# First recurrent layer: both gates in one stream, memory by a scan of six terms, state by a pair scan

## The chip, the core and the metric

The kernel runs on one core of a Trainium2 chip. Five engines matter: PE (matrix products), DVE (vector), ACT (activation functions), POOL (a second vector engine) and SP (which only issues DMAs). Each works off its own instructions in order and waits for the others by semaphores. The metric is the device time of one execution in microseconds (us), the median of several runs.

## The reference

Four layers run one after the other on x of shape (8, 512, 512): batch B = 8, time T = 512, width D = 512. Each adds its output to x. The first three are recurrences over the 512 time steps, the fourth is causal attention with 16 heads. The change touches the first layer:

```python
def step(h, x_t):
    fused = jax.nn.sigmoid(jnp.concatenate([x_t, h], axis=-1) @ w_W + w_b)
    hidden_state, output_state = jnp.split(fused, 2, axis=-1)
    memory_state = x_t @ wx_W + wx_b + hidden_state * (h @ wh_W + wh_b)
    h_new = output_state * h + (1.0 - output_state) * jnp.tanh(memory_state)
    return (h_new, h_new)
```

So a step needs three products of the state h with 512x512 matrices: for the hidden gate, for the output gate, and for the memory. The second and third layers are plain: `h = tanh(x_t @ Wx + b + h @ Wh)`.

## The kernel before

All three recurrences run at the same time, each some steps behind the one before (`OFF = (0, 9, 21)`). One call of `turn(s)` is one time step of each layer that is live at s. Layer 0 is live for s = 0 to 511, layer 1 from s = 9, layer 2 from s = 21, and the loop ends at s = 532. The order of the instructions on PE, DVE, ACT and POOL is the program's own (`manual_schedule`); only the loads and the splitting of weights ahead of the loop are ordered by the scheduler.

The state is float32, but these products are made in bf16: a float32 number is the sum of three bf16 numbers, its upper half and two rests. The state tile `h0` therefore holds four slots per number, [128, 4 chunks, 8 batches, 4 slots], of which three are in use: the number, the number less its upper half (`rest`, line 481), and that less its upper half again. The matmul takes the upper halves of all four slots as 32 columns (8 batches x 4 slots), and the weights are split in three bf16 parts too (`split`, lines 352 to 357, which takes two copies on ACT and two subtractions on DVE for each part of a weight). Four products fill four groups of 32 partitions of one PSUM tile.

What a step does, in the order of the program:
- PE: `ph` (48 matmuls of 256 columns: products of the state for the memory and the hidden gate), `po` (48 of 128 columns: for the output gate), `give0` and `give12` (line 508 and 521: products of x for a coming step), `p12` (48 of 256 columns: the state products of layers 1 and 2), and, from about s = 85 on, three `pieces` of the attention's projections (line 630).
- Layer 0 on DVE, ACT and POOL (lines 720 to 745): `turned` (line 590) transposes `ph` in 32x32 blocks from PSUM to SBUF, so that the four slots' products lie side by side; a fifth number beside them is the bias or x's share; `summed` (line 596) adds the five. A sigmoid gives the hidden gate (736). The same for `po`: `turned`, `summed` into `so`, a sigmoid into `og` (739). A scan over pairs (728) makes memory = gate x sum + x's share; it runs along the row as state = gates x state + term, and a gate of 0 starts each pair anew. Then a tanh (741), `keep` = og x h on POOL (742), `drop` = (og - 1) x tanh on DVE (743), the new state = keep - drop (744), and `rest` twice (481).
- POOL: `place` for the next step (551 twice for layer 0, 555 for layers 1 and 2) adds the biases to x's shares, and 752 adds the new state to x.
- Layers 1 and 2: `turned` of `p12` and `summed` on DVE (behind `rest` of layer 0), four tanh on ACT (763), `rest` on POOL (481), and two additions on POOL (773), the last of them into `xo`.

In POOL's order the additions 773 of one step are followed by `keep` of the next, then by its 551, 551, 555, 752. Every fourth step, `given` (538) transposes the shares of x for the next four steps on DVE.

Of the kernel before, what the change touches and what calls it, by code (L numbers as in the profile page):

```python
# [9 lines left out]
F32 = mybir.dt.float32  # L10
BF16 = mybir.dt.bfloat16
AF = mybir.ActivationFunctionType
ALU = mybir.AluOpType
# [10 lines left out]
NS = 5  # L24
# [10 lines left out]
def cond_residual_kernel(  # L35
# [292 lines left out]
    with ExitStack() as rec:  # L328
# [13 lines left out]
        v0o = wpool.tile([P, KC, 3, D], BF16, name="v0o")  # L342
# [49 lines left out]
        for c in range(KC):  # L392
            stage = stages[c % 3]
            w, r = stage[:, 0 : 3 * D], stage[:, 3 * D :]
            load_rows(nc.sync, w[:, 0:D], wh_w, c)
            load_rows(nc.sync, w[:, D : 2 * D], w_w[D:, 0:D], c)
            load_rows(nc.scalar, w[:, 2 * D :], w_w[D:, D:], c)
            split(v0[:, c], w[:, 0 : 2 * D], r[:, 0 : 2 * D], nc.vector)
            split(v0o[:, c], w[:, 2 * D :], r[:, 2 * D :], nc.vector)
# [40 lines left out]
        s0, s12 = [], []  # L440
        for i in range(2):
            s0.append(wpool.tile([P, 3 * KC, B, NS], F32, name=f"s0_{i}"))
            s12.append(wpool.tile([P, 2 * KC, B, NS], F32, name=f"s12_{i}"))
            nc.vector.tensor_copy(
                s0[i][:, 0:KC, :, NS - 1], bh.unsqueeze(2).to_broadcast([P, KC, B])
            )

        sh = []
        gates = wpool.tile([P, KC, B, 2], F32, name="gates")
        nc.vector.memset(gates, 0.0)
        for i in range(2):
            sh.append(wpool.tile([P, 2 * KC, B, 2], F32, name=f"sh_{i}"))

# [8 lines left out]

        def part(h, i):
            return h[..., i]

        def top(h, i):

            return h.bitcast(BF16)[..., 2 * i + 1]
# [68 lines left out]
        def place(s, layers):  # L540
# [4 lines left out]
            if layers[0] == 0:  # L545
                for to, k in (
                    (s0[s % 2][:, KC:, :, NS - 1], slice(0, 2 * KC)),
                    (sh[s % 2][:, 0:KC, :, 1], slice(2 * KC, 3 * KC)),
# [45 lines left out]
        def summed(to, parts):  # L594

            nc.vector.tensor_reduce(to, parts, AX.X, ALU.add)  # L596
# [103 lines left out]
        def turn(s):  # L700
# [6 lines left out]
            if 0 in now:  # L707
# [3 lines left out]
                stream(po, old0, v0o, 1)  # L711
# [8 lines left out]
            if 0 in now:  # L720
                parts = s0[s % 2]

                def small(name, n=KC):
                    return sp.tile([P, n, B], F32, tag=name, name=f"{name}_{s}")

                def scan(to, q, ab):
                    to, q, ab = (x.rearrange("p c b i -> p (c b i)") for x in (to, q, ab))
                    nc.vector.tensor_tensor_scan(to, q, ab, 0.0, ALU.mult, ALU.add)

                so, og = small("so"), small("og")  # L730
                mem = sp.tile([P, KC, B, 2], F32, tag="mem", name=f"mem_{s}")
                th, keep, drop = small("th"), small("keep"), small("drop")
                hm = sh[s % 2]
                turned(parts[:, 0 : 2 * KC], ph)
                summed(hm[..., 0], parts[:, 0 : 2 * KC])
                nc.scalar.activation(gates[..., 1], hm[:, KC:, :, 0], AF.Sigmoid)  # L736
                turned(parts[:, 2 * KC : 3 * KC], po)
                summed(so, parts[:, 2 * KC : 3 * KC])
                nc.scalar.activation(og, so, AF.Sigmoid)  # L739
                scan(mem, gates, hm[:, 0:KC])  # L740
                nc.scalar.activation(th, mem[..., 1], AF.Tanh)  # L741
                nc.gpsimd.tensor_tensor(keep, og, part(old0, 0), ALU.mult)  # L742
                nc.vector.scalar_tensor_tensor(drop, og, 1.0, th, ALU.subtract, ALU.mult)  # L743
                nc.vector.tensor_tensor(part(new0, 0), keep, drop, ALU.subtract)
# [10 lines left out]
            if later:  # L755
                ps = rows_of(later)
                turned(s12[s % 2][ps], p12[ps])
                s_ = sp.tile([P, 2 * KC, B], F32, tag="s_", name=f"s_{s}")
# [441 lines left out]
```

## Time and profile before

| what | value |
| --- | --- |
| time, median of 3 runs | 3488.78 us (3484.61 to 3498.84) |
| span of the profiled execution | 3484.3 us |
| PE busy | 3313.8 us (95%) |
| PE weight loads busy (beside PE) | 2650.8 us (76%) |
| DVE busy | 2469.7 us (71%) |
| ACT busy | 1434.6 us (41%) |
| POOL busy | 1311.7 us (38%) |
| first transpose of `ph` | 49.71 us |
| last transpose of `ph` (s = 511) | 2656.09 us |

The profile is of one execution. A row of the timeline reads: start, duration, engine, line, operation, output<-inputs, shapes, count, and in brackets how long the engine was idle before and what ended that. A row of the costliest groups gives busy time, mean duration in ns, and idle time ahead of it. Loads and splits fill the first 50 us, the recurrences run from 50 to about 2,700 us, and the rest is attention, which the change does not touch.

### The profile page before, as it was taken

To read this page: it belongs to the slowest core of one execution; us is meant where nothing else is said; L and a number is where in the kernel's file an instruction comes from. 1 tells how busy PE (TensorE), PEld (TensorE's weight loads), DVE (VectorE), ACT (ScalarE), POOL (GpSimd) and SP (SyncE) were. 2 spreads that over 40 slices of the span, in tenths; PEclk is the share of its full clock that TensorE was granted. 3 is DMA by queue.
4 is the path that set the end of the run, shared out by engine and by line. 5 is a ranking of instruction groups with operands and counts; after the bars stand their busy time and mean duration, and the time that the engine had idled before them with its cause. 6 is when DMAs were issued, how large, how long until landed. Compare 5 with 4: busy or idle time off the path is not lost. (4 is left out here: it accounts for less than half of the span.)

```text
span 3484.3 us, 213758 instructions
## 1 busy us (share of the span) xinstructions
PE 3313.8 (95%) x94712; PEld 2650.8 (76%) x94712; DVE 2469.7 (71%) x7411; ACT 1434.6 (41%) x5203; POOL 1311.7 (38%) x4970
## 2 busy tenths in 40 slices
PE   4899999999999999999999999999999879999999
PEld 2677778888888888888888888888886646666666
DVE  4677777777777777777777777777775357777775
ACT  3233333333333333333333333333333257777774
POOL 2444444444444444444444444444443111111110
PEclk9999999999999999999999999999999979999999
DMA  4200000001000100100010001000113121222211
GB/s 128 55 8 8 8 23 17 17 20 29 17 20 18 31 17 17 29 17 17 20 29 17 17 19 29 17 17 17 29 20 64 35 90 47 82 69 65 64 51 26
DMA packets 186565, 114.61 MB, mean 33 GB/s; under 512 B 134220, under 2 KB 165988, under 8 KB 185628
## 3 DMA queue, kind: packets, MB, share of 16 engines
q1 hardware_dynamic: 180056, 96.08, 10.9%
q8 instruction: 743, 12.17, 1.5%
q10 hardware_dynamic: 4992, 2.11, 0.3%
q0 software_dynamic: 592, 2.75, 0.2%
q14 instruction: 182, 1.49, 0.1%
HBM read 59.97 MB, written 40.92 MB: 29 GB/s over the span
## 5 line engine op out<-in xcount | busy, mean ns | idle before, releaser
L565 PEld LDWEIGHTS <-h 128*32 128x32 bf16 x49152 | 1074.0, 97 | 216.6 <-DVE h L481 152.7
L763 ACT ACTIVATE h<-s 64x32 f32<-64x32 f32 x2048 | 537.1, 262 | 1004.9 <-DVE s L596 978.8
L565 PE MATMUL ph<-v,h 128*32 128x256 bf16 x24576 | 796.4, 274 | 59.6 <-DVE h L481 43.8
L581 PE MATMUL p<-v,h 128*32 128x256 bf16 x24576 | 820.2, 273 | 15.6 <-DVE h L481 12.7
L581 PEld LDWEIGHTS <-h 128*32 128x32 bf16 x24576 | 719.5, 97 | 108.7 <-ACT h L763 16.1
L481 POOL TENSOR_TENSOR h<-h 128x64 f32<-128x64 f32 (+1 forms) x1006 | 323.0, 321 | 1152.3 <-ACT h L763 1112.9
L508 PE MATMUL pg<-w0x,xb 128*32 128x384 f32 x4096 | 452.6, 491 | 26.0 <-DMA w0x<-in_wx_W_dram 10.5
L590 DVE STREAM_TRANSPOSE s<-ph 128x256 f32<-128x256 f32 x512 | 230.3, 450 | 346.5 <-PE ph L565 346.4
L565 PE MATMUL po<-v0o,h 128*32 128x128 bf16 x24576 | 469.9, 220 | 6.2 <-issue 5.2
L521 PE MATMUL pg<-w12x,xb 128*32 128x256 f32 x4096 | 349.5, 380 | 9.3 <-DVE raw L538 5.7
L481 DVE TENSOR_TENSOR h<-h 128x32 f32<-128x32 f32 (+1 forms) x1078 | 281.3, 262 | 69.6 <-ACT h L763 32.9
L521 PEld LDWEIGHTS pg<-w12x,xb 128*32 128x32 f32 x4096 | 165.3, 110 | 175.7 <-issue 137.3
L630 PE MATMUL pq<-xo,w_qkv 128*32 128x256 f32 (+2 forms) x4136 | 292.7, 371 | 0.5 <-issue 0.5
L736 ACT ACTIVATE gates<-sh 128x32 f32<-128x32 f32 x512 | 120.3, 235 | 407.4 <-DVE sh L596 403.9
L596 DVE TENSOR_REDUCE sh<-s 128x64 f32<-128x320 f32 x512 | 248.9, 486 | 54.9 <-POOL h L481 2.7
L596 DVE TENSOR_REDUCE s<-s 128x64 f32<-128x320 f32 (+1 forms) x524 | 254.5, 486 | 19.6 <-DVE s L590 0.5
L590 DVE STREAM_TRANSPOSE s<-p 128x256 f32<-128x256 f32 (+1 forms) x524 | 232.6, 444 | 47.3 <-PE p L581 44.4
L742 POOL TENSOR_TENSOR keep<-og,h 128x32 f32<-128x32 f32 x512 | 138.3, 270 | 255.9 <-ACT og L739 255.5
L978 DVE TENSOR_REDUCE rtop<-s 128x1 f32<-128x128 f32 (+7 forms) x384 | 222.1, 599 | 15.1 <-DMA v_out<-ev 5.2
L743 DVE SCALAR_TENSOR_TENSOR drop<-og,th 128x32 f32<-128x32 f32 x512 | 113.7, 222 | 153.8 <-ACT th L741 153.8
L945 PE MATMUL s<-qkt 32*128 32x384 f32 (+3 forms) x1024 | 173.5, 479 | 38.7 <-ACT prob L992 27.2
L1042 ACT COPY pt<-tr 128x512 f32<-128x512 f32 x256 | 135.2, 591 | 153.2 <-PE tr L1037 152.9
(164 smaller groups left out, 4437.4 us busy)
## 6 DMA issues: line engine op xcount, KB each, us to landing
qk_out<-e SPq DMA_DIRECT2D x56, 256.0 KB
qkt<-qk_out SPq DMA_DIRECT2D x14, 960.0 KB
xin<-in_x_dram SPq DMA_DIRECT2D x128, 64.0 KB
xr<-x_out SPq DMA_DIRECT2D x8, 1024.0 KB
out_dram<-res SPq DMA_DIRECT2D x256, 32.0 KB
x_out<-xo SPq DMA_DIRECT2D x28, 256.0 KB
v_out<-ev SPq DMA_DIRECT2D x56, 128.0 KB
vt<-v_out SPq DMA_DIRECT2D x7, 768.0 KB
```

The lines of the kernel that those rows point to most:

```text
L481: eng.tensor_tensor(part(h, i + 1), part(h, i), top(h, i), ALU.subtract)
L508: nc.tensor.matmul(pg[0][j * BP : (j + 1) * BP, :], tokens(t, c), w[:, j], start=(c == 0), stop=(c == KC - 1),)
L521: nc.tensor.matmul(pg[1][q * BP : (q + 1) * BP, :].rearrange("r (v n) -> r v n", v=2), tokens(t, c), w[:, u], start=(c == 0), stop=(c == K ...
L565: nc.tensor.matmul(out[j * BP : (j + 1) * BP, :], half(h, c), w[:, c, i].rearrange("p (g j n) -> p j g n", g=cols, j=KC)[:, j], start=(c = ...
L581: nc.tensor.matmul(out[q * BP : (q + 1) * BP, :].rearrange("r (v n) -> r v n", v=2), half(h[:, l - 1], c), w[:, u], start=(c == 0 and i == 0),
L590: nc.vector.transpose(to[:, :, :, 0 : NS - 1], p.rearrange("p (k b i) -> p k b i", b=B, i=NS - 1))
L596: nc.vector.tensor_reduce(to, parts, AX.X, ALU.add)
L630: nc.tensor.matmul(ps[0][j * BP : (j + 1) * BP, at:end], lhs[:, j * BP : (j + 1) * BP], rhs[:, at:end], start=(k == 0 and at == 0), stop=( ...
L742: nc.gpsimd.tensor_tensor(keep, og, part(old0, 0), ALU.mult)
L763: nc.scalar.activation(part(new12[v * 2 * BP : (v + 1) * 2 * BP, l - 1], 0), s_[fr, v * KC : (v + 1) * KC], AF.Tanh,)
L945: nc.tensor.matmul(pair[g, u, i // 2 * 2][:, i % 2, at : at + n], qkt[b][hs, 0, c, m * P : n], qkt[b][hs, 1, c, 0:n], start=True, stop=False,)
L978: nc.vector.tensor_reduce(top[:, k, 0:n], s[:, :, at : at + (m + 1) * P], AX.X, ALU.max)
```

## The change

For layer 0:
- `ph` now holds both gates and `po` the memory's product: the weight tiles change contents (`v0o` becomes `v0m`), so the split of the 512-wide part takes its data from the `wh` rows, which SP loads, and the wide one from both `w_w` parts, of which ACT loads one.
- One `summed` and one sigmoid (64 columns, not 32 twice) give both gates.
- The products in `po` are no longer summed. They are transposed into `terms`, six numbers for each output: four slots' products, the bias `bh`, and x's share. One scan along 192 elements adds five of them: the gates tile holds 0, 0, 1, 1, 1 and the hidden gate in the six places.
- The new state is made by a second scan over pairs: first the tanh (gate 0), then (1 - og) x tanh + og x h. It writes two slots of the new state's tile, the tanh to slot 0 and the state to slot 2. POOL makes og x h as before, into `kept`, and now also 1 - og, into `drops` (a tensor_scalar with two operations).
- The slots of the state are renumbered (`SLOT`), in all three layers. Slot 0 holds no part of the state now, so `summed` skips it and adds four numbers and not five, also for layers 1 and 2.
- The step's small tiles have one buffer each and not two.

```diff
@@ -339,7 +339,7 @@
         v0 = big.tile([P, KC, 3, 2 * D], BF16, tag="bigB", name="v0")
-        v0o = wpool.tile([P, KC, 3, D], BF16, name="v0o")
+        v0m = wpool.tile([P, KC, 3, D], BF16, name="v0m")
         v12 = wpool.tile([P, 2, KC, 3, D], BF16, name="v12")
         w0x = big.tile([P, KC, 3 * D], F32, tag="bigA", name="w0x")
         w12x = wpool.tile([P, 2, KC, D], F32, name="w12x")
@@ -395,8 +395,8 @@
             load_rows(nc.sync, w[:, 0:D], wh_w, c)
             load_rows(nc.sync, w[:, D : 2 * D], w_w[D:, 0:D], c)
             load_rows(nc.scalar, w[:, 2 * D :], w_w[D:, D:], c)
-            split(v0[:, c], w[:, 0 : 2 * D], r[:, 0 : 2 * D], nc.vector)
-            split(v0o[:, c], w[:, 2 * D :], r[:, 2 * D :], nc.vector)
+            split(v0[:, c], w[:, D:], r[:, D:], nc.vector)
+            split(v0m[:, c], w[:, 0:D], r[:, 0:D], nc.vector)
         load_x(1)
         for i, (wx, wh) in enumerate(((wx1, wh1), (wx2, wh2))):
             for c in range(KC):
@@ -437,23 +437,21 @@
-        s0, s12 = [], []
+        s0, sm, s12 = [], [], []
         for i in range(2):
-            s0.append(wpool.tile([P, 3 * KC, B, NS], F32, name=f"s0_{i}"))
+            s0.append(wpool.tile([P, 2 * KC, B, NS], F32, name=f"s0_{i}"))
+            sm.append(wpool.tile([P, KC, B, NS + 1], F32, name=f"sm_{i}"))
             s12.append(wpool.tile([P, 2 * KC, B, NS], F32, name=f"s12_{i}"))
             nc.vector.tensor_copy(
-                s0[i][:, 0:KC, :, NS - 1], bh.unsqueeze(2).to_broadcast([P, KC, B])
-            )
-
-
-
-
-        sh = []
-        gates = wpool.tile([P, KC, B, 2], F32, name="gates")
-        nc.vector.memset(gates, 0.0)
-        for i in range(2):
-            sh.append(wpool.tile([P, 2 * KC, B, 2], F32, name=f"sh_{i}"))
-
+                sm[i][..., NS - 1], bh.unsqueeze(2).to_broadcast([P, KC, B])
+            )
+
+
+        gates = wpool.tile([P, 2 * KC, B, NS + 1], F32, name="gates")
+        nc.vector.memset(gates, 1.0)
+        nc.vector.memset(gates[..., 0:2], 0.0)
+        drops = wpool.tile([P, KC, B, 2], F32, name="drops")
+        nc.vector.memset(drops, 0.0)
         h0, h12 = [], []
@@ -463,12 +461,14 @@
             nc.vector.memset(h0[i], 0.0)
             nc.vector.memset(h12[i], 0.0)
+        SLOT = (2, 1, 3)
+
         def part(h, i):
-            return h[..., i]
+            return h[..., SLOT[i]]
         def top(h, i):
-            return h.bitcast(BF16)[..., 2 * i + 1]
+            return h.bitcast(BF16)[..., 2 * SLOT[i] + 1]
         def half(h, c):
@@ -544,8 +544,8 @@
             share = raw[min(layers[0], 1), s - r - AHEAD + KC - 1][..., r * B : (r + 1) * B]
             if layers[0] == 0:
                 for to, k in (
-                    (s0[s % 2][:, KC:, :, NS - 1], slice(0, 2 * KC)),
-                    (sh[s % 2][:, 0:KC, :, 1], slice(2 * KC, 3 * KC)),
+                    (s0[s % 2][..., NS - 1], slice(0, 2 * KC)),
+                    (sm[s % 2][..., NS], slice(2 * KC, 3 * KC)),
                 ):
                     bias = bias0[:, k].unsqueeze(2).to_broadcast([P, k.stop - k.start, B])
                     nc.gpsimd.tensor_tensor(to, share[:, k], bias, ALU.add)
@@ -593,7 +593,7 @@
         def summed(to, parts):
-            nc.vector.tensor_reduce(to, parts, AX.X, ALU.add)
+            nc.vector.tensor_reduce(to, parts[..., 1:], AX.X, ALU.add)
         def live(s):
             return [l for l in range(3) if 0 <= s - OFF[l] < T]
@@ -708,7 +708,7 @@
                 ph = pst.tile([P, 2 * P], F32, tag="ph", name=f"ph_{s}")
                 po = pst.tile([P, P], F32, tag="po", name=f"po_{s}")
                 stream(ph, old0, v0, 2)
-                stream(po, old0, v0o, 1)
+                stream(po, old0, v0m, 1)
             if 0 in given_to:
                 give0(s)
             give12(s, [l for l in given_to if l])
@@ -718,30 +718,28 @@
             take(3 if s < T else 12)
             if 0 in now:
-                parts = s0[s % 2]
-
-                def small(name, n=KC):
-                    return sp.tile([P, n, B], F32, tag=name, name=f"{name}_{s}")
+                parts, terms = s0[s % 2], sm[s % 2]
+
+                def small(name, *shape):
+                    return sp.tile([P, *shape, B], F32, tag=name, name=f"{name}_{s}", bufs=1)
                 def scan(to, q, ab):
-                    to, q, ab = (x.rearrange("p c b i -> p (c b i)") for x in (to, q, ab))
+                    q, ab = (x.rearrange("p c b i -> p (c b i)") for x in (q, ab))
                     nc.vector.tensor_tensor_scan(to, q, ab, 0.0, ALU.mult, ALU.add)
-                so, og = small("so"), small("og")
-                mem = sp.tile([P, KC, B, 2], F32, tag="mem", name=f"mem_{s}")
-                th, keep, drop = small("th"), small("keep"), small("drop")
-                hm = sh[s % 2]
-                turned(parts[:, 0 : 2 * KC], ph)
-                summed(hm[..., 0], parts[:, 0 : 2 * KC])
-                nc.scalar.activation(gates[..., 1], hm[:, KC:, :, 0], AF.Sigmoid)
-                turned(parts[:, 2 * KC : 3 * KC], po)
-                summed(so, parts[:, 2 * KC : 3 * KC])
-                nc.scalar.activation(og, so, AF.Sigmoid)
-                scan(mem, gates, hm[:, 0:KC])
-                nc.scalar.activation(th, mem[..., 1], AF.Tanh)
-                nc.gpsimd.tensor_tensor(keep, og, part(old0, 0), ALU.mult)
-                nc.vector.scalar_tensor_tensor(drop, og, 1.0, th, ALU.subtract, ALU.mult)
-                nc.vector.tensor_tensor(part(new0, 0), keep, drop, ALU.subtract)
+                pre = small("pre", 2 * KC)
+                mem = sp.tile([P, KC, B, NS + 1], F32, tag="mem", name=f"mem_{s}", bufs=1)
+                kept = sp.tile([P, KC, B, 2], F32, tag="kept", name=f"kept_{s}", bufs=1)
+                og = gates[:, KC:, :, NS]
+                turned(parts, ph)
+                summed(pre, parts)
+                nc.scalar.activation(gates[..., NS], pre, AF.Sigmoid)
+                turned(terms, po)
+                nc.gpsimd.tensor_tensor(kept[..., 1], og, part(old0, 0), ALU.mult)
+                nc.gpsimd.tensor_scalar(drops[..., 1], og, -1.0, 1.0, ALU.mult, ALU.add)
+                scan(mem.rearrange("p c b i -> p (c b i)"), gates[:, 0:KC], terms)
+                nc.scalar.activation(kept[..., 0], mem[..., NS], AF.Tanh)
+                scan(new0.rearrange("p c b (v two) -> p (c b v) two", two=2)[:, :, 0], drops, kept)
                 rest(nc.vector, new0)
             if 0 in nxt:
                 place(s + 1, [0])
@@ -755,7 +753,7 @@
             if later:
                 ps = rows_of(later)
                 turned(s12[s % 2][ps], p12[ps])
-                s_ = sp.tile([P, 2 * KC, B], F32, tag="s_", name=f"s_{s}")
+                s_ = sp.tile([P, 2 * KC, B], F32, tag="s_", name=f"s_{s}", bufs=1)
                 summed(s_[ps], s12[s % 2][ps])
                 for l in later:
                     fr = rows_of([l])
```

## The prediction

> **What bounds the kernel now.** I read the busy tenths first, then windows, the waits, and last the timeline of single steps. The recurrences fill 50 to 2,660 us, and only there does the change touch anything that repeats. Two stretches differ:
>
> ```profile
> core 0: us, PE busy (x) PEld busy (x) DVE busy (x) ACT busy (x) POOL busy (x), PEclk, DMA share, GB/s
> 200.00:400.00 200.00, 184.56 (x6484) 146.17 (x6476) 151.89 (x466) 71.67 (x285) 93.80 (x365) 1.00 0.03 9
> 1000.00:1500.00 500.00, 496.49 (x16753) 418.47 (x16743) 365.14 (x1123) 179.09 (x706) 228.93 (x881) 1.00 0.09 22
> ```
>
> Columns: the stretch, then busy time of each engine. In the first PE is idle 15 of 200 us, in the second 3.5 of 500, and the clock is 1.00 in both. From step 85 on PE also works off pieces of the attention projections (`take`). The starts of PE's groups in the timeline give its full step: ph 1.31 + po 0.67 + pg0 0.65 + pg12 0.43 + p12 1.31 + pieces 0.65 = 5.01 us. Between starts of the 128x256 transpose of ph I find 5.01 to 5.02 in over half the steps after 110, mean 5.11. So PE sets those; of 418 steps from 90 to 508, 104 start ph within 0.12 us of the end of the second L481, that is, wait for the state, and these exceed 5.01 by 11.2 us together. The other excess (31.5 us) is PE waiting on its own issue, as in `PEld pg L521 <- issue` here, and stays.
>
> ```profile
> engine line waited for: us in total, times, longest us
> PEld pg L521 <- issue: 48.7, 262, 0.7
> PEld L565 <- DVE h L481: 36.0, 117, 0.6
> ```
>
> Before step 85 there are no pieces, PE needs 4.37, and the step takes 4.93 on average (4.79 or 4.94): there the chain of layer 0 sets the time. One such step, times in us:
>
> ```profile
> 306.50 0.45 DVE L590 STREAM_TRANSPOSE s<-ph 128x256 f32<-128x256 f32 x1 [0.73 <-PE ph L565]
> 307.05 0.48 DVE L596 TENSOR_REDUCE sh<-s 128x64 f32<-128x320 f32 x1
> ...
> 307.63 0.23 ACT L736 ACTIVATE gates<-sh 128x32 f32<-128x32 f32 x1 [0.65 <-DVE sh L596]
> ...
> 307.80 0.32 DVE L596 TENSOR_REDUCE so<-s 128x32 f32<-128x160 f32 x1
> ...
> 307.95 0.27 POOL L773 TENSOR_TENSOR xo<-xb,h 128x32 f32<-128x32 f32 x1
> ...
> 308.40 0.23 ACT L741 ACTIVATE th<-mem 128x32 f32<-128x32 f32 x1
> 308.51 0.28 POOL L742 TENSOR_TENSOR keep<-og,h 128x32 f32<-128x32 f32 x1 [0.29 <-ACT og L739]
> ...
> 308.96 0.22 DVE L744 TENSOR_TENSOR h<-keep,drop 128x32 f32<-128x32 f32 x1
> ...
> 309.21 0.47 DVE L481 TENSOR_TENSOR h<-h 128x32 f32<-128x32 f32 x2
> 309.22 0.39 POOL L555 TENSOR_TENSOR s<-raw,bias 128x64 f32<-128x64 f32 x1
> ```
>
> I count from the transpose, 306.50 = 0. The first L481 starts at 2.71, the second ends at 3.18, PE starts ph at 3.24, and its transpose follows 1.55 later: 4.79. In 53% of steps the first L481 takes 0.37 and not 0.22: L555 on POOL has started up to 3 ns before it. Where it starts 2 ns after, DVE takes 0.22 and L555 0.40 and not 0.31. Whoever comes first makes the other wait.
>
> **The chain after the change, with each engine left alone.** The sum of four terms: rows of 320 and 160 elements take 486 and 320 ns, so 1.04 ns an element and 153 ns fixed; 256 take 0.42, ending at 0.97. The sigmoid over 64 columns: +0.10 to start; 262 ns, because the copies of 512 and 1024 elements (0.62, 1.04) give 0.83 ns an element and 32 more add 27 to 235. It ends at 1.33. The transpose of po runs meanwhile (0.88 to 1.19). The scan of 192 elements has no row; 64 take 0.286. With the fixed 153 of the reduce, 64 elements cost 133, 2.08 each, and 192 take 0.55. Ends: 0.42 at the reduce's 1.04 an element, 0.86 in proportion; I take 0.55, since every DVE row here has a fixed part. It runs 1.37 to 1.92, the tanh ends at 2.18, and the pair scan (64 elements, 0.286) could run 2.22 to 2.51; L481 would start at 2.55 against 2.71. Off the chain go the sum `so` (0.32), the second sigmoid, `drop` and `sub`.
>
> **What POOL makes of it.** `keep` moves from 2.01 (where POOL had nothing to do) to right behind the sigmoid, under the long scan, and `drops` follows it; both end the chain now, since the pair scan reads them. `drops` is a tensor_scalar: 128x4 takes 237 ns, 128x512 1,493, so 32 columns 0.31 (low end 0.25, as a tensor_tensor of 32; high 0.38 for two operations). The startup shows how POOL and DVE meet:
>
> ```profile
> 61.45 1.15 POOL L357 TENSOR_TENSOR v<-w_qkv,v 128x512 bf16<-128x512 f32 x1 [2.46 <-ACT v L356]
> 61.66 0.99 DVE L743 SCALAR_TENSOR_TENSOR drop<-og,th 128x32 f32<-128x32 f32 x1 [0.34 <-ACT th L741]
> ```
>
> A 0.22 us DVE instruction takes 0.99: it ends 0.05 after POOL's. The other way round I have only L555 behind a short L481 (its data pass then begins some 0.035 after DVE ends). The Trainium skill (SBUF — State Buffer, "Who interferes with whom") says that a DVE instruction with two SBUF inputs and a GpSimd one that reads SBUF exclude each other for the whole instruction, the first one winning: by it `keep` waits out the whole scan, while by the weakest reading of the rows it would lose only the 0.09 that L555 lost.
>
> I take the waiting in full. *Case C*, POOL free when the sigmoid ends: keep's pass starts when the scan ends and ends at 2.03 (0.07 of its 0.27 is the pass); drops 2.00 to 2.31; POOL issues the next L551 at 2.26, just ahead of the pair scan at 2.34, so that ends only 0.14 after L551, at 2.71; L481 2.75 to 2.97; L555 is queued by 2.79 and goes next, to 3.15; the second L481 ends at 3.20. Before: 3.18 or 3.33. So nothing is gained in the chain and little lost.
>
> *Cases A and B*: POOL arrives late. In the steps without pieces the second L773 ends at 1.72 (measured), now 1.65 with the shorter reduce of layers 1 and 2, so it starts at 1.38, against the scan's 1.37. If the scan wins (A), L773 ends at 2.03, keep and drops at 2.55, the pair scan at 2.95 and the second L481 at 3.45. If L773 wins (B), the scan ends at 2.05, drops at 2.44, L481 at 3.34. Steps: 1.55 + 0.06 + those = 5.06 or 4.95, against 4.93. Below nothing: if POOL and DVE didn't hinder each other at all, the second L481 ends at 3.03 and a step is 4.64.
>
> **The startup.** The instruction order of the changed kernel shows another edit: the 512-wide split (now `v0m`) waits for SP's `wh` rows. In the old order its four splits ran between 16.1 and 28.2 us while the loads of `wh` and `w_w` were under way; now each stands ahead of the wide split of its chunk, behind ACT's 24 bias issues. A chunk then goes through ACT and DVE in turns: 0.69 + 0.62 + 1.04 + 1.23 + 1.04 + 1.23 us and five handovers of 0.04 = 6.05; four from 29.6 (ACT's 36 issues at about 0.5 us from 10.9, and one 0.62 copy) end at 53.8; the last one now ends at 49.2. That is +4.6 (0 if the issues end early, 7 if the last chunk's loads slip too). No DMA is added, and the queues' issues are the same in number.
>
> **The sum**, against the profile's 3484.3 us:
> - startup +4.6
> - steps 0 to 20 (PE waits, at most one later layer, so case C: +0.07 each) +1.4
> - steps 21 to 84: midway between A and B, 64 x 0.07 = +4.5
> - steps 85 to 511: PE sets 5.01. PE-bound, POOL is ahead (the transpose comes 1.67 behind ph's start, not 1.55), so case C: 1.67 + 0.06 + 3.20 = 4.93 fits under 5.01 with 0.08 to spare. Of the 11.2 us that the state now costs I give back half: -5
> - the 21 steps after layer 0 ends: the reduce is 0.066 shorter, -1.4
> - buffers cut to one copy: nothing; each is read some 3 us before it is written again, and if not it shows as a DVE wait.
>
> +4.1: 3488.4. The median shown is 4.5 above this execution, so I put 3493. Less than 0.5% (17 us) can't be told from no change.
>
> **The rivals.**
> 1. *Slower, chance 0.38: the long scan and POOL lock in case A.* It is self-consistent: in chain-bound steps the turn of layers 1 and 2 on DVE and POOL hangs on the second L481, so POOL is late by the same amount in each step. Then the steps with pieces take 5.06 against 5.01: 427 x 0.045 = +19, steps 21 to 84 +8, startup and first steps +6, end -1: +32, 3521 on the median's scale. It decides once L773 starts behind the scan. For: 1.38 against 1.37. Against: PE-bound steps pull POOL ahead. With a scan of 0.86, C in those steps is 1.55 + 0.06 + 3.51 = 5.12: another +0.11 x 427 = 47.
> 2. *Faster, chance 0.14: POOL and DVE overlap.* 4.64 against 4.93 in 85 steps, -25, and all of the 11 us; startup +4.6, end -1: -32, 3457. Against: the row of 0.99.
> 3. *The chain doesn't matter at all*, PE covers both: only the startup remains, 3493. It falls into my forecast.
>
> **How the numbers follow.** No change: 0.48, with its own range of 3480 to 3505. Slower by over 0.5%: 0.38. Faster by over 0.5%: 0.14. The range reaches from part of rival 2 (3466) to rival 1 with half of the dear scan (3545).
>
> **What would show it.** The scan's row should read near 0.55; `keep` should run from the sigmoid into 2.03 and look long (0.6); the pair scan should start on POOL and not on the tanh; steps of 5.01 should prevail after 85; the first ph transpose should start near 54 us, not 49.7. A scan near 0.42, or a `keep` of 0.27 under a running scan, proves me wrong towards faster; steps of 5.1 without pieces and no floor at 5.01, towards slower.

## The result and the profile after

The changed kernel takes 3504.9 us (median of six runs, 3501.3 to 3507.8), the kernel before 3490.4 us (3484.6 to 3498.8) in runs taken beside it. The ratio is 1.0036, with a 95% interval of 1.0023 to 1.0050: some 13 us slower, measurable, but under the 0.5% that the prediction calls no change. The profiled spans (3505.1 and 3484.3) are 20.8 us apart, the medians 14.5, since the profile of before lies 6 us below its median and that of after at its own. Where the 20.8 us arise is read from the starts of the 128x256 transpose of `ph`:

| | before | after | difference | added since the row above |
| --- | --- | --- | --- | --- |
| step 0 | 49.7 | 55.3 | +5.6 | +5.6 |
| step 21 | 163.5 | 175.4 | +11.9 | +6.3 |
| step 85 | 478.9 | 497.5 | +18.6 | +6.7 |
| step 511 | 2656.1 | 2672.9 | +16.8 | -1.8 |
| end | 3484.3 | 3505.1 | +20.8 | +4.0 |

So almost everything is lost before step 85, in the sixth of the loop where the attention's pieces don't yet cover the chain. The windows of the changed kernel, in the columns and stretches shown before:

```profile
200.00:400.00 200.00, 181.08 (x6372) 143.69 (x6364) 140.71 (x378) 67.36 (x242) 110.06 (x400) 1.00 0.03 7
1000.00:1500.00 500.00, 497.77 (x16896) 400.44 (x16892) 348.08 (x932) 177.19 (x613) 275.69 (x984) 1.00 0.09 22
```

In the first PE (the first pair) does less in 200 us than before (6372 matmuls against 6484). DVE (third) is less busy, by 11.2 us, and POOL (fifth) more, by 16.3 us: work went from the one to the other, and the step still got longer. In the second PE is as full as before. The waits between 1000 and 2000 us, the stretch that the prediction's two rows come from:

```profile
PEld pg L521 <- issue: 63.8, 327, 1.0
PEld L565 <- DVE h L481: 63.1, 154, 0.8
DVE h L728 <- POOL drops L739: 60.9, 153, 0.6
```

PE's wait for the state has gone from 36.0 to 63.1 us, and a row is new: the pair scan that makes the state waits for `drops` on POOL. These weight loads wait beside running matmuls, so most of this time costs nothing. Counted as in the prediction (steps that start `ph` within 0.12 us of the end of the second L481), 363 of the 418 steps from 90 to 508 now wait for the state, against 104, and lose 20.6 us to it against 11.2; the rest of the excess over 5.01, PE's own issue, is 18.4 here against 31.5. Part of it may now fall into the time in which PE waits anyway, but that is not shown: e1 below, whose loop has the same instructions, loses about as much to the state and more to its own issue, so that it takes 2184.6 us from step 85 to 511, where this profile has 2175.3 and that of before 2177.2. The step stays at its floor: median 5.017 in both, mean 5.10 against 5.11.

One step without pieces, timeline of the changed kernel (PE and most of layers 1 and 2 left out; L771 is line 773 of before):

```profile
311.38 0.45 DVE L590 STREAM_TRANSPOSE s<-ph 128x256 f32<-128x256 f32 x1 [0.43 <-PE ph L565]
...
311.94 0.42 DVE L596 TENSOR_REDUCE pre<-s 128x64 f32<-128x256 f32 x1
...
312.45 0.33 ACT L736 ACTIVATE gates<-pre 128x64 f32<-128x64 f32 x1 [0.66 <-DVE pre L596]
...
312.77 0.27 POOL L771 TENSOR_TENSOR xo<-xb,h 128x32 f32<-128x32 f32 x1
312.87 0.58 DVE L728 TENSOR_TENSOR_SCAN mem<-gates,sm 128x192 f32<-128x192 f32 x1 [0.29 <-ACT gates L736]
...
313.00 0.55 POOL L738 TENSOR_TENSOR kept<-gates,h 128x32 f32<-128x32 f32 x1
313.48 0.27 ACT L741 ACTIVATE kept<-mem 128x32 f32<-128x32 f32 x1 [0.70 <-DVE mem L728]
313.52 0.24 POOL L739 TENSOR_SCALAR drops<-gates 128x32 f32<-128x32 f32 x1
313.73 0.31 POOL L551 TENSOR_TENSOR s<-raw,bias 128x64 f32<-128x64 f32 x1
313.86 0.31 DVE L728 TENSOR_TENSOR_SCAN h<-drops,kept 128x64 f32<-128x64 f32 x1 [0.41 <-POOL drops L739]
313.98 0.25 POOL L551 TENSOR_TENSOR sm<-raw,bias 128x32 f32<-128x32 f32 x1
314.18 0.31 POOL L555 TENSOR_TENSOR s<-raw,bias 128x64 f32<-128x64 f32 x1
314.20 0.59 DVE L481 TENSOR_TENSOR h<-h 128x32 f32<-128x32 f32 x2
```

`kept` needs 0.30 us ahead of a scan, as in the next timeline (`keep` in the kernel before: 0.27). Here it is issued 0.13 after the scan and ends 0.10 after the scan's end at 313.45. `drops` follows it and ends at 313.76, no sooner than the tanh (313.75), so POOL is as late as the chain itself. Its two L551 still follow, and so L555 starts at 314.18, just ahead of L481, which takes 0.59 for both and not 0.47. Counted from the transpose, the second L481 ends at 3.41; the prediction had 3.34 for case B and 3.45 for case A. The steps without pieces (25 to 83) take 5.03 us on average, median 5.01, against 4.93.

But this meeting of L555 and L481 is no cost of the change. The step of the kernel before that the prediction shows (L481 at 309.21) is one of the fewer in which DVE came first. The step ahead of it, timeline of the kernel before:

```profile
304.03 0.22 DVE L744 TENSOR_TENSOR h<-keep,drop 128x32 f32<-128x32 f32 x1
...
304.28 0.30 POOL L555 TENSOR_TENSOR s<-raw,bias 128x64 f32<-128x64 f32 x1
304.28 0.61 DVE L481 TENSOR_TENSOR h<-h 128x32 f32<-128x32 f32 x2
```

Over steps 25 to 83 the first L481 takes more than 300 ns in 43 of 59 steps before and in 54 of 59 after. On average over steps 25 to 82 the balance is this. The memory scan starts 0.05 us earlier and takes 0.26 longer (0.59 for 0.33). From its end to the instruction that makes the state it is 0.20 less, since `drop` is gone. That instruction, now the pair scan, takes 0.09 more (0.32 for 0.23), and the two L481 take 0.59 for 0.58. So the two longer scans cost 0.35 us, the shorter sums and the missing `drop` save 0.25, and the rest is the 0.10 us that such a step lost.

Where POOL has nothing to do when the sigmoid ends, the order is the other one. Timeline of the changed kernel again, a step of the second stretch:

```profile
1513.79 0.32 ACT L736 ACTIVATE gates<-pre 128x64 f32<-128x64 f32 x1 [0.78 <-DVE pre L596]
...
1514.20 0.72 DVE L728 TENSOR_TENSOR_SCAN mem<-gates,sm 128x192 f32<-128x192 f32 x1 [0.28 <-ACT gates L736]
1514.20 0.30 POOL L738 TENSOR_TENSOR kept<-gates,h 128x32 f32<-128x32 f32 x1
1514.47 0.49 POOL L739 TENSOR_SCALAR drops<-gates 128x32 f32<-128x32 f32 x1
...
1514.95 0.26 ACT L741 ACTIVATE kept<-mem 128x32 f32<-128x32 f32 x1 [0.84 <-DVE mem L728]
...
1515.31 0.29 DVE L728 TENSOR_TENSOR_SCAN h<-drops,kept 128x64 f32<-128x64 f32 x1 [0.40 <-POOL s L551]
```

Both are issued at 1514.20. Now `kept` is short (0.30) and the scan pays, 0.72 against a median of 0.56; `drops` then stands behind the scan (0.49 against 0.24). `kept` starts no later than the scan in 20 of 20 steps between 50 and 170 us, in 5 of 59 without pieces, and in 98 of 411 with pieces.

### The profile page after: what moved, and what is told of

The parts are those of the page before. It is cut to its first block, busy times and chain, and to the rows that moved or that the text cites. A ratio compares the mean times of both kernels' runs of the same rounds, so it can differ in the third digit from the quotient of the medians.

```text
span 3505.1 us, 211743 instructions
## 1 busy us (share of the span) xinstructions
PE 3320.4 (95%) x94712; PEld 2581.0 (74%) x94712; DVE 2372.8 (68%) x6389; ACT 1415.4 (40%) x4691; POOL 1546.2 (44%) x5482
## 3 DMA queue, kind: packets, MB, share of 16 engines
q0 software_dynamic: 592, 2.75, 0.2%
q14 instruction: 167, 1.37, 0.1%
## 5 line engine op out<-in xcount | busy, mean ns | idle before, releaser
L565 PEld LDWEIGHTS <-h 128*32 128x32 bf16 x49152 | 1038.1, 97 | 269.1 <-DVE h L481 214.8
L481 POOL TENSOR_TENSOR h<-h 128x64 f32<-128x64 f32 (+1 forms) x1006 | 320.8, 319 | 1142.4 <-ACT h L761 1103.0
L581 PEld LDWEIGHTS <-h 128*32 128x32 bf16 x24576 | 700.9, 97 | 125.4 <-ACT h L761 15.4
L565 PE MATMUL po<-v0m,h 128*32 128x128 bf16 x24576 | 453.7, 220 | 4.0 <-issue 3.3
L728 DVE TENSOR_TENSOR_SCAN mem<-gates,sm 128x192 f32<-128x192 f32 x512 | 306.9, 599 | 150.3 <-ACT gates L736 147.6
L481 DVE TENSOR_TENSOR h<-h 128x32 f32<-128x32 f32 (+1 forms) x1078 | 291.9, 272 | 69.7 <-ACT h L761 33.6
L736 ACT ACTIVATE gates<-pre 128x64 f32<-128x64 f32 x512 | 165.8, 324 | 379.2 <-DVE pre L596 377.0
L728 DVE TENSOR_TENSOR_SCAN h<-drops,kept 128x64 f32<-128x64 f32 x512 | 161.6, 316 | 204.8 <-POOL drops L739 152.0
L738 POOL TENSOR_TENSOR kept<-gates,h 128x32 f32<-128x32 f32 x512 | 261.0, 510 | 63.4 <-ACT gates L736 55.8
L521 PEld LDWEIGHTS pg<-w12x,xb 128*32 128x32 f32 x4096 | 145.3, 110 | 189.9 <-issue 165.8
L741 ACT ACTIVATE kept<-mem 128x32 f32<-128x32 f32 x512 | 134.1, 262 | 370.5 <-DVE mem L728 370.5
L596 DVE TENSOR_REDUCE pre<-s 128x64 f32<-128x256 f32 x512 | 215.0, 420 | 54.6 <-POOL h L481 2.3
L596 DVE TENSOR_REDUCE s<-s 128x64 f32<-128x256 f32 (+1 forms) x524 | 219.9, 420 | 19.3
```

Source lines behind the costliest of these rows:

```text
L481: eng.tensor_tensor(part(h, i + 1), part(h, i), top(h, i), ALU.subtract)
L521: nc.tensor.matmul(pg[1][q * BP : (q + 1) * BP, :].rearrange("r (v n) -> r v n", v=2), tokens(t, c), w[:, u], start=(c == 0), stop=(c == K ...
L565: nc.tensor.matmul(out[j * BP : (j + 1) * BP, :], half(h, c), w[:, c, i].rearrange("p (g j n) -> p j g n", g=cols, j=KC)[:, j], start=(c = ...
L581: nc.tensor.matmul(out[q * BP : (q + 1) * BP, :].rearrange("r (v n) -> r v n", v=2), half(h[:, l - 1], c), w[:, u], start=(c == 0 and i == 0),
L596: nc.vector.tensor_reduce(to, parts[..., 1:], AX.X, ALU.add)
L738: nc.gpsimd.tensor_tensor(kept[..., 1], og, part(old0, 0), ALU.mult)
```

## The experiments

Two sets, each on one chip with its own runs of the kernel before beside it (24 in the first, 20 in the second). Ratios are to those; the changed kernel's own is the one given above, and it was not run again in these sets. First their numbers together, in us where not said otherwise; the last four columns are from the one profiled execution of each.

| kernel | ratio, 95% interval | first transpose of `ph` | mean step, 25 to 83 | step 85 at | step 511 at |
| --- | --- | --- | --- | --- | --- |
| before | 1 | 49.7 | 4.93 | 478.9 | 2656.1 |
| after | 1.0036 (1.0023 to 1.0050) | 55.3 | 5.03 | 497.5 | 2672.9 |
| e1, wh rows by ACT | 1.0023 (1.0008 to 1.0039) | 49.8 | 5.04 | 491.6 | 2676.2 |
| e2, POOL's order | 1.0009 (0.9998 to 1.0021) | 55.5 | 4.89 | 489.1 | 2665.5 |
| e3, no scan of six | 0.9961 (0.9945 to 0.9976) | 54.8 | 4.83 | 475.5 | 2646.4 |
| e4, before with four-term sums | 0.9957 (0.9943 to 0.9971) | 50.1 | 4.83 | 472.0 | 2642.7 |
| e5, e4 with POOL's order | 0.9954 (0.9937 to 0.9971) | 49.4 | 4.76 | 468.7 | 2649.5 |
| e6, e3 with e1's and e2's edits | 0.9965 (0.9947 to 0.9982) | 49.4 | 4.84 | 473.8 | 2664.6 |
| e7, `drops` by ACT | 1.0006 (0.9992 to 1.0021) | 55.6 | 4.91 | 488.1 | 2674.2 |
| e8, before with `og` spread out | one run | 50.0 | 4.97 | 483.9 | 2673.1 |

For the steps without pieces the chain can be compared directly: medians over steps 25 to 82, in us from the transpose of `ph`.

| | memory scan starts | ends | state starts (pair scan; 744 in before, e4, e5) | first L481 starts | second L481 ends |
| --- | --- | --- | --- | --- | --- |
| before | 1.53 | 1.87 | 2.47 | 2.72 | 3.34 |
| after | 1.48 | 2.06 | 2.46 | 2.82 | 3.41 |
| e2 | 1.48 | 2.05 | 2.45 | 2.78 | 3.25 |
| e3 | 1.65 | 2.04 | 2.41 | 2.74 | 3.21 |
| e4 | 1.43 | 1.80 | 2.39 | 2.65 | 3.23 |
| e5 | 1.43 | 1.72 | 2.35 | 2.60 | 3.08 |
| e7 | 1.42 | 2.07 | 2.47 | 2.80 | 3.27 |

From step 85 to 511 the single profiles differ by up to 20 us (2170.7 for e4, 2190.8 for e6) for reasons of PE's own issue, so that small gains are read at step 85 and the ratio alone decides on the whole.

### e1: the split no longer behind SP's rows

```diff
-            load_rows(nc.sync, w[:, 0:D], wh_w, c)
+            load_rows(nc.scalar, w[:, 0:D], wh_w, c)
             load_rows(nc.sync, w[:, D : 2 * D], w_w[D:, 0:D], c)
-            load_rows(nc.scalar, w[:, 2 * D :], w_w[D:, D:], c)
+            load_rows(nc.sync, w[:, 2 * D :], w_w[D:, D:], c)
```

> The changed kernel with one edit: ACT loads the wh rows and SP both w_w parts, so that the 512-wide split again has the data that ACT loads early. Theory (the startup lost its 5.6 us because each narrow split now stands ahead of its chunk's wide one): the scheduler puts the narrow splits ahead again, the first transpose of ph starts near 49.7 us and not 55.3, everything after keeps its lead, time 5.6 us under the changed kernel (near 3499). Rival (the first steps wait for the weights of layers 1 and 2 anyway): the first transpose is earlier, but step 32 is reached as late as now (230.6 us) and the time stays near 3505.

The first transpose moves from 55.3 to 49.8, the difference is still 5.9 us at step 85, and the step without pieces stays at 5.04. The startup's price in the profile is settled. In the time of the whole it is not: the interval overlaps that of the changed kernel, and at step 511 e1's profile is 3.3 us behind (2676.2 against 2672.9).

The changed kernel's startup shows why (timeline, ACT's DMA issues under ACTq):

```profile
27.67 3.08 ACTq L430 DMA_DIRECT2D bias<-in_b_dram  x5
...
30.87 0.62 ACT L354 COPY v0m<-stage 128x512 bf16<-128x512 bf16 x1 [21.80 <-DMA bias<-in_b_dram]
...
32.77 1.04 ACT L354 COPY v<-stage 128x1024 bf16<-128x1024 bf16 x1
32.89 0.69 DVE L357 TENSOR_TENSOR v0m<-stage,v0m 128x512 bf16<-128x512 f32 x1 [0.68 <-ACT v0m L356]
33.84 1.23 DVE L355 TENSOR_TENSOR stage<-stage,v 128x1024 f32<-128x1024 f32 x1 [0.26 <-ACT v L354]
```

ACT does nothing but issue DMAs for 21.80 us, and only then begins the first narrow split, with the wide one of the same chunk behind it. In the kernel before, the four narrow splits were done by 28.2.

### e2: POOL's order

```diff
+            if 0 in now:
+                x = xb[s // TB][:, :, s % TB, :]
+                nc.gpsimd.tensor_tensor(x, x, part(new0, 0), ALU.add)
             if 0 in nxt:
                 place(s + 1, [0])
             if [l for l in nxt if l]:
                 place(s + 1, [l for l in nxt if l])
-            if 0 in now:
-                x = xb[s // TB][:, :, s % TB, :]
-                nc.gpsimd.tensor_tensor(x, x, part(new0, 0), ALU.add)
```

> The changed kernel with one edit: POOL adds the new state to x ahead of the three additions of place, so that those fall into POOL's idle time and not beside the pair scan and L481. Theory (DVE and POOL exclude each other, so POOL's neighbours of the chain lengthen it): L481 is 0.22 us in nearly all steps, the pair scan 0.29, a step without pieces falls from 5.01 to about 4.85, step 85 is reached some 11 us earlier, time near 3494. Rival (the long scan and ACT's slower sigmoid and tanh alone make the chain longer): 5.01 stays, 3505.

Mean step 4.89, median 4.85, step 85 comes 8.4 us earlier than in the changed kernel, and the ratio's interval lies below its. Timeline of e2, a step whose transpose starts at 307.90:

```profile
309.38 0.59 DVE L728 TENSOR_TENSOR_SCAN mem<-gates,sm 128x192 f32<-128x192 f32 x1 [0.28 <-ACT gates L736]
309.51 0.55 POOL L738 TENSOR_TENSOR kept<-gates,h 128x32 f32<-128x32 f32 x1
...
310.04 0.24 POOL L739 TENSOR_SCALAR drops<-gates 128x32 f32<-128x32 f32 x1
310.36 0.29 DVE L728 TENSOR_TENSOR_SCAN h<-drops,kept 128x64 f32<-128x64 f32 x1 [0.40 <-POOL drops L739]
310.69 0.47 DVE L481 TENSOR_TENSOR h<-h 128x32 f32<-128x32 f32 x2
```

Nothing was taken out: POOL still does the same six instructions. But the one behind `drops` now waits for the state, so POOL is quiet while DVE makes it: the pair scan takes 0.29 and not 0.32 (medians), the two L481 take 0.47 and not 0.59, and the second ends at 3.26 from the transpose, not 3.41. `kept` still waits out the scan (0.55), and the scan ends where it did (2.05 and 2.06 in the table): of the 0.16 us, 0.12 are won at the two L481 and 0.03 at the pair scan. The two L481 (0.47) are now shorter than in the kernel before (0.61), so most of this is a new gain, and not the return of what the change lost.

### e3: the change without the scan of six

The products in `po` and the bias are summed ahead of the scan, over four terms, and memory is made by a scan over pairs; one stream for both gates, one sigmoid, the pair scan for the state and the four-term sums stay.

```diff
-            sm.append(wpool.tile([P, KC, B, NS + 1], F32, name=f"sm_{i}"))
+            sm.append(wpool.tile([P, KC, B, NS], F32, name=f"sm_{i}"))
+            sh.append(wpool.tile([P, KC, B, 2], F32, name=f"sh_{i}"))
...
-        gates = wpool.tile([P, 2 * KC, B, NS + 1], F32, name="gates")
-        nc.vector.memset(gates, 1.0)
-        nc.vector.memset(gates[..., 0:2], 0.0)
+        gates = wpool.tile([P, 2 * KC, B, 2], F32, name="gates")
+        nc.vector.memset(gates, 0.0)
...
                 turned(terms, po)
+                summed(sh[s % 2][..., 0], terms)
...
-                scan(mem.rearrange("p c b i -> p (c b i)"), gates[:, 0:KC], terms)
-                nc.scalar.activation(kept[..., 0], mem[..., NS], AF.Tanh)
+                scan(mem.rearrange("p c b i -> p (c b i)"), gates[:, 0:KC], sh[s % 2])
+                nc.scalar.activation(kept[..., 0], mem[..., 1], AF.Tanh)
```

> The changed kernel without the scan of six terms: po's products and bias are summed (reduce of four terms, under the sigmoid), then a scan over pairs as before. The rest of the change stays. Theory (the long scan holds POOL's kept and drops back, and these end the chain): kept is 0.2 us shorter, the pair scan starts 0.15 to 0.2 earlier but still on drops, a step without pieces is about 4.83, time near 3492. Chain alone, with no port between the engines: the tanh would end it, a step is about 4.68, time near 3483. If the scan of six were free: 5.01, 3505.

The steps without pieces come to 4.83, as expected of the first theory, and the ratio turns: 0.9961. Timeline of e3, a step whose transpose starts at 306.55:

```profile
307.61 0.27 ACT L736 ACTIVATE gates<-pre 128x64 f32<-128x64 f32 x1 [0.67 <-DVE pre L596]
...
307.78 0.29 DVE L596 TENSOR_REDUCE sh<-sm 128x32 f32<-128x128 f32 x1
...
308.16 0.29 POOL L739 TENSOR_TENSOR kept<-gates,h 128x32 f32<-128x32 f32 x1
308.19 0.40 DVE L728 TENSOR_TENSOR_SCAN mem<-gates,sh 128x64 f32<-128x64 f32 x1
308.41 0.22 POOL L740 TENSOR_SCALAR drops<-gates 128x32 f32<-128x32 f32 x1
...
308.96 0.29 DVE L728 TENSOR_TENSOR_SCAN h<-drops,kept 128x64 f32<-128x64 f32 x1 [0.37 <-POOL s L551]
...
309.29 0.47 DVE L481 TENSOR_TENSOR h<-h 128x32 f32<-128x32 f32 x2
```

The table tells where this comes from, and it is not where I looked. The sum (0.29) starts under the sigmoid but outlasts it, so the scan starts 0.17 later than in the changed kernel; being shorter it ends at 2.04, against 2.06. In the chain the six-term scan and the sum with a pair scan cost the same. The difference is POOL's: `kept` starts ahead of the scan (in 58 of 61 such steps), `drops` is done at 308.63, the L551 run under the tanh, and L555 is under way before L481, which takes 0.47. The second L481 ends 0.20 sooner: 0.04 by the earlier start of the pair scan, 0.03 by its own length (0.29) and 0.12 at L481. In the first steps, too, the undisturbed step takes 4.70 instead of 4.97, and of the 418 steps from 90 to 508 only 12 still wait for the state, and lose 0.7 us by it. Part of the 0.20 may not be the scan's: e3 also brings the gates from 24 to 8 bytes apart, and with that the sigmoid from 324 to 269 ns and the tanh from 262 to 237 (see e8). What these two are worth by themselves in the step was not tried.

### e4: the sums over four terms alone, on the kernel before

```diff
+        SLOT = (2, 1, 3)
+
         def part(h, i):
-            return h[..., i]
+            return h[..., SLOT[i]]
...
-            return h.bitcast(BF16)[..., 2 * i + 1]
+            return h.bitcast(BF16)[..., 2 * SLOT[i] + 1]
...
-            nc.vector.tensor_reduce(to, parts, AX.X, ALU.add)
+            nc.vector.tensor_reduce(to, parts[..., 1:], AX.X, ALU.add)
```

> The kernel before with one part of the change: the slots of the state renumbered, so that all sums go over four numbers and not five. Theory: a reduce of 256 elements takes 0.42 and not 0.49 us, one of 128 elements 0.29 and not 0.32; about 0.1 us of the chain goes, a step without pieces falls from 4.93 to about 4.83, step 85 comes 8 us earlier, and the steps with pieces wait less for the state: 8 to 15 us under the kernel before (3475 to 3482). Rival (the chain is hidden): the time of before, 3490.

4.83, and 0.9957 for the whole, 15 us. This small part is the gain of the change. e3, which holds it too, stands where e4 does (0.9961, the intervals overlap): what one stream for both gates and the pair scan add to it, less what the later start takes, can't be measured.

### e5: e4 with POOL's order

The edits of e4 and e2 on the kernel before.

> The kernel before with the sums over four terms, and POOL's addition of the new state to x (752) put ahead of its additions of the biases (551, 555). Theory (two-input instructions of POOL and DVE keep each other off): with the four-term sums alone the steps without pieces took 4.83 us and the first subtraction of rest (481) was still long where 555 came first; with the order changed 481 stays near 0.23 us in all steps and the steps come to about 4.73 to 4.75; over the run another 5 to 10 us, so a ratio of about 0.993 to 0.9945 to the kernel before. Rival (the order only helped because drops stood late in the changed kernel): 4.83 stays, the ratio stays at 0.9957.

The steps without pieces fall further, to 4.76 on average and 4.68 in the median, so the order acts without `drops` too and the rival's 4.83 falls. The whole does not show it: 0.9954 against 0.9957, where 0.993 to 0.9945 was expected. Step 85 is reached 3.3 us earlier than in e4, less than the interval can tell. At the end of the second L481 the order wins 0.15 us here (3.23 to 3.08) and 0.16 in the changed kernel (e2): it helps either kernel alike. No kernel tried is measurably better than e4; e5 has the lowest ratio.

### e6: e3 with both other edits

> The changed kernel without the scan of six terms (products summed, memory by a scan over pairs), with the load of the wh rows by ACT and POOL's addition to x ahead of the bias additions. Theory (the three costs are separate: the long scan, the turn of POOL, the split behind SP's rows): the first transpose of ph near 49.8 us, steps without pieces near 4.73, and the gains add up: ratio to the kernel before about 0.992 (0.9961 less 0.0013 for the loads less 0.0027 for the order). Rival (the gains hang on the same wait and do not add): not below 0.995.

The first transpose is at 49.4, but the step is 4.84 where 4.73 was expected, and the ratio 0.9965: the rival was right, the gains don't add up. Two reasons can be read. In e3 the mean L481 was 220 ns already: with the scan of six gone POOL no longer stood in its way, and the order had nothing left to mend. And of the 5.4 us gained at the start 2.3 are left at step 12 and 1.7 at step 85. After step 85 the state costs 0.9 us in all, while PE's waits for its own issue are 54 us in this profile against 35 in e3; why they differ is open. The profile of e6 is also of the slowest of its nine runs (3507.7 us, median 3489.0).

### e7: `drops` by ACT

```diff
-                nc.gpsimd.tensor_scalar(drops[..., 1], og, -1.0, 1.0, ALU.mult, ALU.add)
+                nc.scalar.activation(drops[..., 1], pre[:, KC:], AF.Sigmoid, scale=-1.0)
```

> The changed kernel with 1 - og made by ACT as a sigmoid of the negated sums and no longer by POOL. Theory (the long scan and what POOL runs beside it cost the time, drops only passes the delay on): the pair scan then waits for the tanh and meets POOL's 551, which moves up by the length of drops; it starts 0.05 to 0.1 us earlier, steps without pieces about 4.95 us against 5.03, ratio to the kernel before 1.001 to 1.003. Rival (POOL's added instruction is the cost of the change): steps without pieces fall to about 4.83 as without the scan of six, ratio about 0.997.

4.91 and 1.0006: a little better than the first theory had it, and far from the rival's 4.83 and 0.997. Timeline of e7, a step whose transpose starts at 306.65:

```profile
308.07 0.62 DVE L728 TENSOR_TENSOR_SCAN mem<-gates,sm 128x192 f32<-128x192 f32 x1 [0.22 <-ACT drops L739]
308.23 0.56 POOL L738 TENSOR_TENSOR kept<-gates,h 128x32 f32<-128x32 f32 x1
308.72 0.26 ACT L741 ACTIVATE kept<-mem 128x32 f32<-128x32 f32 x1 [0.69 <-DVE mem L728]
308.75 0.31 POOL L551 TENSOR_TENSOR s<-raw,bias 128x64 f32<-128x64 f32 x1
309.01 0.25 POOL L551 TENSOR_TENSOR sm<-raw,bias 128x32 f32<-128x32 f32 x1
309.09 0.31 DVE L728 TENSOR_TENSOR_SCAN h<-drops,kept 128x64 f32<-128x64 f32 x1 [0.40 <-POOL s L551]
```

The pair scan now waits for POOL's L551 as the first theory says, but it starts where it did (2.47 and 2.46 in the table) and not 0.05 to 0.1 earlier. POOL, however, is through earlier, and L481 takes 0.47 again. That gives back 0.12 of the 0.20 us that e3 gives, so `drops` had more part in it than I allowed. It is one of three ways to the same end: in the steps without pieces (25 to 83) the mean L481 takes 275 ns in the changed kernel and 219 or 220 ns in e2, e3 and e7. The kernel before has 271, e4 257 and e5 221.

### e8: `og` spread out

```diff
-                so, og = small("so"), small("og")
+                so = small("so")
+                og = sp.tile([P, KC, B, 6], F32, tag="og", name=f"og_{s}", bufs=1)[..., 5]
```

> The kernel before, with only og's place changed: its 32 numbers a partition stand 24 bytes apart and not 4. Theory (ACT pays for the distance between the numbers, some 1 ns an element at 24 bytes): the sigmoid into og takes about 0.26 us, while the sigmoid into gates (8 bytes apart) and the tanh stay at 0.23. Rival (the sigmoid of the changed kernel is long because of 64 columns alone): all three stay at 0.23 to 0.24.

The groups of instructions between 200 and 2600 us in e8 (its lines stand one below those of before; behind the first bar busy us and mean ns):

```profile
L740 ACT ACTIVATE og<-so 128x32 f32<-128x32 f32 x469 | 123.9, 264 | 160.4 <-DVE so L596 96.4 <-POOL xo L774 61.1 <-DVE mem L728 2.5
L737 ACT ACTIVATE gates<-sh 128x32 f32<-128x32 f32 x469 | 110.9, 236 | 351.3 <-DVE sh L596 350.1 <-DVE s L590 1.1
L743 POOL TENSOR_TENSOR keep<-og,h 128x32 f32<-128x32 f32 x469 | 143.7, 306 | 223.3 <-ACT og L740 221.2 <-ACT th L742 2.1
```

The sigmoid into `og` goes from 230 to 264 ns, the one into `gates` (8 bytes apart) stays at 236 and the tanh at 233, and `keep` on POOL, which reads `og`, goes from 270 to 306: about 1.1 ns an element on both engines. The step without pieces follows, 4.97 against 4.93.

## Why the prediction held, step by step

The forecast, no change that can be told, was right, with the time at its edge: 3493 forecast, 3504.9 measured, inside the forecast's own 3480 to 3505. That it lies inside, by 0.1 us, is luck: the sum behind it was +4.1 us; the profiles show +20.8, the medians +14.5. The startup, the exclusion of POOL and DVE and the floor of 5.01 were right. The terms for steps 0 to 20, for steps 85 to 511 and for the end were mis-sized, and that for steps 21 to 84 came out in part for other reasons than those given.

- **Startup, +4.6; measured +5.6.** The mechanism and nearly the size. ACT's issues ended at 30.7, so the first split began at 30.87 and not 29.6; the chunks then took 5.8 us rather than 6.05, and the first transpose came at 55.3 where 54 was forecast. e1 took exactly this away.
- **Steps 0 to 20, +1.4; measured +6.3. This term was mis-sized.** Case C has `kept` behind the scan and the chain 0.07 longer. With POOL idle `kept` starts first instead, in all 20 steps looked at, and the scan and `drops` pay as at 1514.20: an undisturbed step takes 4.97 against 4.74, 0.23 each and not 0.07, some 3 us over the 14 such steps. Another 1.3 is step 0, where the second `ph` takes 2.75 and not 1.49, at a granted clock of 1.00 in both; why is open (e3 and e1 have it, e7 has not). The rest lies in steps that POOL disturbs with work I had not costed, the splits of weights of layers 1 and 2. In both kernels four of them hit DVE; before they hit `drop` (0.99 each, the row at 61.66 that the prediction shows), now L481. Timeline of the changed kernel, step 8:

```profile
102.29 1.49 DVE L481 TENSOR_TENSOR h<-h 128x32 f32<-128x32 f32 x2
102.31 1.14 POOL L357 TENSOR_TENSOR v<-w_qkv,v 128x512 bf16<-128x512 f32 x1
...
103.83 2.60 PE L565 MATMUL ph<-v,h 128*32 128x256 bf16 x48 [2.74 <-DVE h L481]
```

  The two L481 take 1.49 for 0.47; PE waits 2.74 us and then needs 2.60 for a `ph` that takes 1.49 elsewhere, at a granted clock of 0.63 between 103 and 107 us. The step takes 7.08. This was read, not tried by itself.
- **Steps 21 to 84, +4.5; measured +6.7.** The bracket of A and B held: 5.03 on average, 5.01 in the median, between 4.95 and 5.06 and nearer A. In part this is luck. Both cases end the pair scan later than it was (A at 2.95, B, worked back from its 3.34, at 2.83; measured 2.78), and both leave L481 at 0.47, where it took 0.59. The prediction read the long L481 of the kernel before, but its cases for the kernel after have none. Nearly every `kept` (54 of 59) stands behind the scan, but L771 wins its turn ahead of it, 1.39 against 1.49 from the transpose: POOL came when I had it (1.38), the scan later than I had it (1.37). The scan itself was priced well, 0.55 for a median of 0.56 between 200 and 2600 us (0.58 in these steps, behind L771). What I had too small was ACT: the sigmoid 324 ns for 262, the tanh 262 for 230, and 0.09 from the sigmoid to the scan, where I put 0.04. e8 names a cause for the first, the distance of 24 bytes between the numbers that it writes; the tanh reads at that distance, and takes 237 ns at 8 bytes in e3.
- **Steps 85 to 511, -5; measured -1.8. This term was mis-sized too.** PE sets the step, as predicted: 5.017 in the median in both kernels. Case C was to leave 0.08 us of room and half the 11.2 us. Instead the chain of 3.41 and the 1.55 to 1.67 before it make 5.02 to 5.14, as long as PE's step, and 363 of 418 steps wait for the state; it costs 20.6 us and not half of 11.2. That the whole stretch is still 1.8 us shorter says little: PE's own issue costs 13 us less in this profile, and e1's loop, which is the same, takes 9 us more. e3, with the chain 0.20 shorter, has 12 such steps and loses 0.7 us.
- **After layer 0, -1.4; measured +4.0.** Up to the last product of layers 1 and 2 the loss grows by 0.8 us, so the 1.4 did not show; 3 of the 4 us arise in the attention behind it, which the change does not touch and which takes 703.1 to 714.3 us in the ten profiles. Between 2700 and 2900 us the granted clock is 0.82 in this profile and 0.85 in the other; e3 and e4, faster kernels, have 0.81 and 0.82 there, so it says nothing about the change.
- **Single buffers, nothing.** None of the waits read points to them; it was not tried by itself.

The exclusion of POOL and DVE, on which the sum and both rivals turned, is shown: `kept` takes 0.55 behind a scan and 0.30 ahead of it, and then it is the scan that grows. So the rule of the Trainium skill (SBUF — State Buffer, "Who interferes with whom") holds here, and not the weak reading by the 0.09 that L555 lost. Rival 2, an overlap, falls. Rival 1 was right in kind. Its price was too high, since with pieces POOL is ahead in a quarter of the steps and the floor of 5.01 covers most of the rest. And its place was off: I had POOL's lateness end in the pair scan, by way of `kept` and `drops`. But `drops` ends with the tanh, and the pair scan starts where line 744 did (2.46 and 2.47). What POOL costs there is 0.03 us of the pair scan's 0.32 (0.29 in e2 and e3). The larger meeting comes one instruction later, where L555 meets L481, and it was there before the change.

## What to carry to other kernels

An instruction given to POOL, or one on DVE made longer, is not priced by the chain alone: follow POOL's queue to the next place where both read SBUF, because the later of the two pays there. And look for such a meeting in the kernel before, too, ahead of blaming the change for it. Here the meeting of L555 and L481 cost some 0.11 us a step on average in both kernels (0.58 and 0.59 for 0.47), and moving POOL's addition of x forward takes it away in either (e2, e5). What the change lost is in the chain: two longer scans cost 0.10 us more than the shorter sums and the missing `drop` save. Additions folded into a scan that waits for the gate cost what the sum cost that could start before the gate was known (the scan ends at 2.06 with them and at 2.04 without, e3). And try each part of a composite change alone: the least conspicuous one, sums over four terms and not five, made the kernel 0.43% faster, and the rest took it back.

## What the runs showed of the hardware

- The distance between the numbers costs on ACT and POOL: 24 bytes instead of 4 add 34 to 36 ns to 32 elements (e8), and the sigmoid of 64 columns takes 324 ns at 24 bytes and 269 at 8 (e3). A distance of 8 bytes costs little: 235 against 230. The Trainium skill (SBUF — State Buffer, "Door 1: The DMA port swizzle") says that accesses which leave a 16-byte line each time pay a penalty; both measured distances fall on the side it gives them, but 16 bytes itself was not tried.
- The scan takes 281 ns for 64 elements and 560 for 192 (medians), 2.18 ns an element on top of 142 ns, twice the reduce's 1.04.
- A tensor_scalar on POOL is kept off by the scan like an instruction with two inputs: `drops` takes 0.24 alone and 0.49 behind the scan.
